# A two-layer graph network kernel: no clearing of the accumulator by GpSimd, seventeen groups gathered from x, and a longer ring of row buffers

## The chip, the cores and the metric

The kernel runs on one core of one Trainium2 chip, as one program. The metric is device microseconds of one execution; the chip's engines are TensorE (PE), VectorE (DVE), ScalarE (ACT), GpSimd (POOL) and SyncE (SP), and DMAs are issued from the queues of SP, ScalarE and GpSimd. Times of before are the median of three executions; the profile is one further execution.

## The reference

There are N = 12,500 nodes of 128 float32 features and 200,000 edges, sorted by their destination `dst`. Cut to what matters:

```
h     = relu(layernorm(x))
w     = edge_weight / segment_sum(edge_weight, dst)[dst]
feat  = relu(h @ W_pool + b_pool)
neigh = segment_max(feat[src] * w, dst)           # layer 1: largest message
r     = h @ W1_self + neigh @ W1_neigh + b1
h1    = relu(r / norm(r))
neigh2 = segment_sum(h1[src] * w, dst) / max(deg, 1)   # layer 2: mean of messages
out   = x + relu(h1 @ W2_self + neigh2 @ W2_neigh + b2)
```

Nodes without edges get 0 in place of the maximum.

## The kernel before

**Groups.** The edges are taken in 391 groups of G = 512 (the last has 320), each as four chunks of 128. For a chunk GpSimd issues one indirect DMA (`gather`, L446): 128 rows of 512 bytes of a table in HBM, chosen by one column of `srcT`, land in one quarter of a row buffer of 128x4x128 float32. Layer 1 gathers from `feat_d`, layer 2 from `h_d`; both tables are written by the kernel. Since the edges are sorted, a group touches a window of at most LW = 48 consecutive nodes; `bases` holds where each window begins.

**Preparation.** A hand-ordered loop of 28 turns (`tc.manual_schedule()`: the order of the program is the order on each engine) runs over 25 node groups of 4x128 nodes. In turn i it does the statistics of node group i (L571 to L576), the normalised rows `xn` and their transposes for i-1 (L554 to L562), `hT` and the product with `W_pool` for i-2 (L546 to L550), and `feat` for i-3, with its store to `feat_d` from SP (L541, L542). The rows of x are loaded into `agg` itself, seen as `xs`; once the rows of a node group are read, GpSimd sets these columns to zero (L563), since `agg` is later the accumulator over nodes. In between, the turns carry steps of three side jobs: `edges1` for the first quarter of the edges, `sources` (turns the source numbers, which lie in `w2T`, into `srcT`; first quarter in turns 0 and 1, the rest in turns 9 to 14) and the loads of the other inputs.

**Raw groups.** `feat_d` is complete only at the end of the preparation. So the first FIRST = 14 groups are gathered from x, which is there from the start: two or three chunks in each turn from turn 2 on, after the turn's clearing. These groups are turned into features on the way (`raw_stats`, `raw_norm`, `raw_columns`, `raw_back`, `raw_product`), at a cost in VectorE, ScalarE and TensorE.

**Layer 1.** A loop of one step per group: ScalarE scales the gathered rows (L868), TensorE transposes them (L869), VectorE takes the running maximum along the edges with a scan (L877), picks the last edge of each node (L885, L886), and a product with a selection matrix (L897, L926) gives 48 columns which ScalarE copies into `agg` at the window's place (`window_copy`, L819). When all windows of 128 nodes are in, `nodes1` computes their `h` and stores it to `h_d`. From step FIRST on, two of three steps also take a `side_step`, which carries on the jobs of `background()`: `edges1` for the other quarters, then `edges2`, `edges3` and `fitness`. `fitness` writes flags into `bad`; where one is set, a slow general path runs at the end of the kernel.

**Row loads beside the gathers.** For every tenth group (sixth in layer 2) `Rows` loads the first chunk row by row with 128 DMAs of 512 bytes from SP and ScalarE (L689), whose addresses come from a small tile `ri` (L672 to L685).

**The ring.** A gather waits until its row buffer has been read. There are RING = 8 own buffers and 8 borrowed ones in tiles that are filled only later: two in `locT`, one each in `lastT` and `invT`, four in `w2T`. Layer 1 uses all 16 for groups below LESS = 64 and the first 8 from there on; layer 2 uses 8. On VectorE's queue and ScalarE's, step i's work waits for the gather of group i; GpSimd's queue is a list of gathers that runs ahead of the steps by as much as the ring lets it.

**Small tiles.** `work(name)` gives single tiles `r_<name>`. The keep flags of groups 0 and 1 lie in `r_f1` (`kt_first`) and the edge weights of group 0 in `r_f0` (`w_first`) until steps 0 to 2 have read them.

Of the kernel before, what the change touches and what calls it, by code (L numbers as in the profile page):

```python
# [7 lines left out]
F32 = mybir.dt.float32  # L8
# [5 lines left out]
OP = mybir.AluOpType  # L14
# [4 lines left out]
P = 128  # L19
D = 128  # L20
G = 512
Q = 4
LW = 48
# [6 lines left out]
ROW_SHIFT = 9  # L30
BL = 8
XC = 8
FIRST = 14
RING = 8
WIDE = 2 * RING
LESS = 64


@with_exitstack
def gnn_kernel(ctx, tc, x, src, dst, ew, w_pool, b_pool, w1s, w1n, b1, w2s, w2n, b2, out):  # L40
# [13 lines left out]
    nc = tc.nc  # L54
    N = x.shape[0]
# [6 lines left out]
    NT = -(-NG // P)  # L62
# [12 lines left out]
    agg = const.tile([P, NP + LW], F32)  # L75
    srcT = const.tile([P, NT, Q, P], I32)
    ewT = const.tile([P, NT, Q, P], F32)
# [12 lines left out]
    rp = both.enter_context(tc.tile_pool(name="rows", bufs=1))  # L90
# [17 lines left out]


    ring = [gp.tile([P, Q, D], F32, name=f"gt{k}") for k in range(RING)]  # L110
    lent = locT.bitcast(F32)
    ring += [lent[:, t:t + 2].rearrange("p t q n -> p (t q n)").rearrange("p (q d) -> p q d", d=D) for t in (0, 2)]
    ring += [a[:, 2:4].rearrange("p t q n -> p (t q) n") for a in (lastT, invT)]
    ring += [w2T[:, t] for t in range(NT)]
    assert len(ring) == WIDE and LESS % WIDE == 0

    def buffer(g, wide):
        return ring[g % (WIDE if wide and g < LESS else RING)]


    dr = rp.tile([P, NT, G + 2], I32)
# [22 lines left out]
    xs = agg[:, :NP].rearrange("p (t d) -> p t d", d=D)  # L144
# [55 lines left out]
    sums = rp.tile([P, NT + 2], F32)  # L200
    counts = rp.tile([P, NT + 2], F32)
    heads = rp.tile([P, NT + 2], F32)
    bad = rp.tile([P, NT, 5], F32)
    for tl in (sums, counts, heads):
        nc.vector.memset(tl, 0.0)
    ones_r = rp.tile([P, G], BF16)
# [2 lines left out]
    def work(name, n=G, dtype=F32):  # L209
        return rp.tile([P, n], dtype, name=f"r_{name}")  # L210
# [27 lines left out]
    def at_pairs(out, f, op):  # L238
        nc.vector.tensor_reduce(out, pairs(f), axis=AX.X, op=op)
# [135 lines left out]
    def fitness(get, t):  # L375

        before, cur, behind = (dr[:, t, i:i + G] for i in range(3))
        begin = work("first", 1)
        nc.vector.tensor_copy(begin, cur[:, 0:1])
        pn = beside(get, cur)  # L380
        yield
        wrong = work("goes", dtype=BF16)
        nc.vector.tensor_tensor(wrong, pn, before, OP.is_lt)
        yield
        nc.vector.tensor_reduce(bad[:, t, 0:1], wrong, axis=AX.X, op=OP.max)
        yield
        loc = work("f1")
        nc.vector.tensor_scalar(loc, pn, float(N - 1), begin, op0=OP.min, op1=OP.subtract)
        last = work("last", dtype=BF16)
        yield  # L390
        nc.vector.tensor_tensor(last, pn, behind, OP.not_equal)
        yield
        nc.vector.tensor_scalar(wrong, loc, float(LW - 1), None, op0=OP.is_gt)
        yield
        nc.vector.tensor_reduce(bad[:, t, 1:2], wrong, axis=AX.X, op=OP.max)
        yield

        one = work("one", 1)
        nc.vector.tensor_tensor(one, before[:, 0:1], behind[:, G - 1:G], OP.is_equal)
        real = work("real", 1)  # L400
        nc.vector.tensor_scalar(real, begin, float(PAST), None, op0=OP.is_lt)
        nc.vector.tensor_tensor(bad[:, t, 2:3], one, real, OP.mult)
        nc.vector.tensor_tensor(bad[:, t, 3:4], begin, need[:, t:t + 1], OP.is_lt)
        yield

        at_pairs(loc[:, :G // 2], last, OP.min)
        yield
        nc.vector.tensor_reduce(bad[:, t, 4:5], loc[:, :G // 2], axis=AX.X, op=OP.max)
# [29 lines left out]
        ne = G if g < GF else TAIL  # L438
        return *divmod(g, P), ne, [(j, min(P, ne - j * P)) for j in range(-(-ne // P))]

    def gather(gt, table_d, g, byrow=None, only=None):
        t, r, ne, chunks = edges_of(g)
        for j, k in chunks if only is None else chunks[only:only + 1]:
            if j == 0 and byrow and byrow.takes(g):
                continue
            nc.gpsimd.indirect_dma_start(  # L446
                out=gt[:k, j, :], out_offset=None, in_=table_d[:, :],
                in_offset=bass.IndirectOffsetOnAxis(ap=srcT[:k, t, j, r:r + 1], axis=0))
        return gt


    gts = {}
# [43 lines left out]
    rest = load_rest()  # L496
    groups = list(node_groups())
    offs, rstds, pts, pfs = ({} for _ in range(4))
    raw_chunks = [(r, j) for r in range(FIRST) for j in range(Q)]

    def split_bias():

# [29 lines left out]
    for i in range(len(groups) + 3):  # L532
        at = [groups[i - k] if 0 <= i - k < len(groups) else None for k in range(4)]
        if at[3]:
            t0, n = at[3]
            pf = pfs.pop(i - 3)
            fr = wk.tile([P, Q, D], F32, name="fr", bufs=3)
            if i % 4 == 3:
                nc.scalar.activation(fr[:, :n, :], pf[:, :n, :], AF.Relu)
            else:  # L540
                nc.vector.tensor_scalar(fr[:, :n, :], pf[:, :n, :], 0.0, None, op0=OP.max)  # L541
            nc.sync.dma_start(feat_d[t0 * P:(t0 + n) * P, :].rearrange("(q p) d -> p q d", p=P),  # L542
                              fr[:, :n, :])
        if at[2]:
            t0, n = at[2]
            nc.scalar.activation(hT[:, t0:t0 + n, :], pts.pop(i - 2)[:, :n, :], AF.Copy)  # L546
            pf = pfs[i - 2] = ps.tile([P, Q, D], F32, name="pf")
            nc.tensor.matmul(pf[:, :n, :], ones_r[0:3, :P], bias_rows[0:3, :n, :], start=True, stop=False)
            for q in range(n):
                nc.tensor.matmul(pf[:, q, :], hT[:, t0 + q, :], W["pool"], start=False, stop=q == n - 1)  # L550
        if at[1]:
            t0, n = at[1]
            rstd = rstds.pop(i - 1)
            nc.vector.reciprocal(rstd, rstd)  # L554
            off = wk.tile([P, Q], F32, name="off")
            nc.vector.tensor_tensor(off, offs.pop(i - 1), rstd, OP.mult)
            xn = wk.tile([P, Q, D], F32, name="xn")
            pt = pts[i - 1] = ps.tile([P, Q, P], F32, name="pt")
            for q in range(n):
                nc.scalar.activation(xn[:, q, :], xs[:, t0 + q, :], AF.Relu, bias=off[:, q:q + 1],  # L560
                                     scale=rstd[:, q:q + 1])
                nc.tensor.transpose(pt[:, q, :], xn[:, q, :], ident)  # L562
            nc.gpsimd.memset(xs[:, t0:t0 + n, :], 0.0)  # L563
        if at[0]:
            t0, n = at[0]
            mv = wk.tile([P, Q, 2], F32, name="mv")
            if n < Q:
                nc.vector.memset(mv, 1.0)
            for q in range(n):
                st = wk.tile([P, 6], F32, name="st")  # L570
                nc.vector.bn_stats(st, xs[:, t0 + q, :])  # L571
                nc.vector.bn_aggr(mv[:, q, :], st)
            rstd = rstds[i] = wk.tile([P, Q], F32, name="rstd")
            nc.scalar.activation(rstd, mv[:, :, 1], AF.Sqrt, bias=eps)
            offs[i] = ps.tile([P, Q], F32, name="neg")
            nc.vector.tensor_scalar(offs[i], mv[:, :, 0], -1.0, None, op0=OP.mult)  # L576
        if 2 <= i < 22:
            next(first_edges, None)
        if i >= 6:
            next(rest, None)  # L580
        if i == 1:
            bias_rows = split_bias()
        if i < 2 or 9 <= i < 15:
            next(source_steps, None)
        if i >= 2:
            n = 2 + (i % 4 == 2) if i < len(groups) else len(raw_chunks)
            for r, j in raw_chunks[:n]:
                gts[r] = gather(buffer(r, True), x, r, only=j)
            raw_chunks = raw_chunks[n:]
        if i == len(groups) - 1:  # L590
            w_first, kt_first = (rp.tile([P, G], F32, name=f"r_f{k}") for k in range(2))
            kt_first = kt_first.bitcast(BF16).rearrange("p (two n) -> p two n", two=2)
            weight_rows(0, w_first)
            keep_rows(0, kt_first)
        k = i - len(groups)
        if k == 1:
            raw_scale(0)
            raw_norm(0)
            raw_columns(pq, 0)
        if k == 2:  # L600
            raw_back(0)
            raw_product(pq, 0)
            nc.scalar.activation(gts[0], raws.pop(0), AF.Relu, bias=bp_col)
            raw_scale(1)
            raw_norm(1)
        if 0 <= k < 3:
            raw_stats(k)
# [180 lines left out]
    with tc.manual_schedule(), tc.tile_pool(name="ew", bufs=3) as wk, \  # L788
# [47 lines left out]
        byrow = Rows(wk, feat_d, 10, [(nc.sync, 96, 16), (nc.scalar, 32, 4)], 30, NG - 16)  # L836
        for i in range(max(turn) + 6):
# [23 lines left out]
            elif i < NG:  # L861
                t, r, ne, chunks = edges_of(i)
                gs = wk.tile([P, G], F32, name="gs", bufs=2).rearrange("p (q d) -> p q d", d=D)
                pms[i] = ps.tile([P, G], F32, name="pm")
                gt = gts.pop(i)
# [7 lines left out]
            g = i - 1  # L873
            if 0 <= g < NG:
# [3 lines left out]
                                             op0=OP.add, op1=OP.max)  # L878
# [13 lines left out]
            g = i - 3  # L892
            if 0 <= g < NG:
                t, r, ne, chunks = pairs_of(g)
# [14 lines left out]
            g = i - 2  # L909
# [7 lines left out]
            g = i - 4  # L917
# [25 lines left out]
        i = NG  # L943
# [172 lines left out]
```

## Time and profile before

| | us |
|---|---|
| median of three executions | 5949.51 (5947.85 to 5975.21) |
| the profiled execution, its own time | 3844.75 |
| its span | 3843.0 |
| last store of `feat_d` issued / first gather from `feat_d` | 96.6 / 101.9 |
| last gather of layer 1 / first of layer 2 | 1940.3 / 1957.9 |
| GpSimd busy | 2873.2, in 3061 instructions |

The profiled execution is far shorter than the timed ones; the page and the trace don't show why. Its mean granted TensorE clock was 0.52: near full in the first 100 us, 0.50 from 600 us on. In the page each digit of a row of slices is the busy share of a fortieth of the span in tenths. A group of instructions is told by line, engine, operation, result and operands, its count, busy time in sum and mean of one in ns, then the idle time of that engine just before and what ended it. An indirect DMA's busy time on GpSimd is the time in which GpSimd handles it; when its data land is seen at those who wait for them.

### The profile page before, as it was taken

Reading aid. Unit: us, or ns where it says so; the run is one execution under the profiler, and the core shown is the slowest. Engines: PE = TensorE matmul, PEld = TensorE weight load, DVE = VectorE, ACT = ScalarE, POOL = GpSimd, SP = SyncE. Lnnn points to the kernel's source line nnn. Section 1 sums busy time; section 2 is a strip of 40 time slices with the busy share of each in tenths; the row PEclk is TensorE's granted clock in tenths of the full one; section 3 lists DMA queues with packets and bytes.
Section 4 is the critical chain, followed back from the end, with each engine's and each line's share of the span. In section 5 each row is a group of like instructions: output and inputs, shape, how many; then the busy total and the mean of one; then the engine's idle time right before and its main releaser. Section 6 shows DMA issues by size and latency. Waiting matters only on the chain.

```text
span 3843.0 us, 61269 instructions
## 1 busy us (share of the span) xinstructions
PE 2317.6 (60%) x8402; PEld 1790.5 (47%) x8402; DVE 1712.7 (45%) x4882; ACT 882.9 (23%) x2996; POOL 2873.2 (75%) x3061
## 2 busy tenths in 40 slices
PE   7666566666666666666655555555555555555555
PEld 5455454444444444444444444444444444444444
DVE  8877666666666666555542222222222222222221
ACT  7644444444444444444410000000000000000000
POOL 6777777777777777777767777777777777777776
PEclk9655555555555555555555555555555555555555
DMA  7433333323333333333312222222222222222222
GB/s 204 122 91 90 87 89 89 89 83 84 86 86 86 86 86 85 85 85 85 84 52 63 62 64 62 62 63 63 63 63 63 62 63 63 63 63 63 63 63 57
DMA packets 224215, 299.55 MB, mean 78 GB/s; under 512 B 70418, under 2 KB 147444, under 8 KB 223798
## 3 DMA queue, kind: packets, MB, share of 16 engines
q0 software_dynamic: 96864, 198.51, 19.8%
q1 hardware_dynamic: 115766, 93.43, 8.5%
q10 hardware_dynamic: 11168, 3.61, 0.6%
q14 instruction: 345, 2.83, 0.2%
q8 instruction: 72, 1.18, 0.1%
HBM read 275.50 MB, written 19.77 MB: 77 GB/s over the span
## 4 chain that ended last, share of the span: by engine, by line
DMA 55%; issue 11%; POOL 8%; PE 7%; DVE 6%; SPq 5%; ACT 4%; ACTq 3%; POOLq 0%; DVEq 0%
DMA gt<-h_d,srcT 33%; DMA gt<-feat_d,srcT 20%; POOL gt L446 8%; PE pa L985 3%; SPq L689 3%; ACTq L689 2%; ACT gs L868 2%; DVE pm L877 2%; PE pm L869 1%; SPq L685 1%; PE pn L739 1%; ACTq L685 1%; PE pn L735 1%; DVE sc L886 1%; DVE sel L897 1%
## 5 line engine op out<-in xcount | busy, mean ns | idle before, releaser
L446 POOL DMA_INDIRECT gt<-h_d,srcT x1499 | 1415.3, 944 | 474.1 <-issue 217.6
L446 POOL DMA_INDIRECT gt<-feat_d,srcT x1371 | 1295.2, 945 | 418.3 <-DMA gt<-feat_d,srcT 165.4
L985 PE MATMUL pa<-s,gt 128*128 128x48 f32 x2998 | 962.3, 425 | 809.2 <-DMA gt<-h_d,srcT 730.4
L985 PEld LDWEIGHTS pa<-s,gt 128*128 128x128 f32 x2998 | 749.7, 312 | 1024.3 <-DMA gt<-h_d,srcT 812.3
L869 PE MATMUL pm<-ident,gs 128*128 128x128 f32 x1507 | 573.0, 463 | 640.2 <-ACT gs L868 557.3
L877 DVE TENSOR_TENSOR_SCAN pm<-kt,carry,pm 128x512 f32<-128x512 bf16 x389 | 499.7, 1285 | 480.7 <-PE pm L869 473.7
L869 PEld LDWEIGHTS pm<-ident,gs 128*128 128x128 f32 x1507 | 284.0, 193 | 877.4 <-ACT gs L868 742.6
L994 DVE TENSOR_TENSOR agg<-pa,agg 128x48 f32 x391 | 81.2, 208 | 1351.6 <-PE pa L985 950.2
L868 ACT ACTIVATE gs<-gt,ewT 128x128 f32<-128x128 f32 x1371 | 489.6, 395 | 584.9 <-DMA gt<-feat_d,srcT 433.6
L926 PEld LDWEIGHTS pa<-sel,rows 128*128 128x128 f32 x1556 | 365.8, 324 | 51.7 <-ACT agg L819 51.3
L926 PE MATMUL pa<-sel,rows 128*128 128x48 f32 x1556 | 369.1, 385 | 17.1 <-ACT agg L819 16.4
L914 PE MATMUL pr<-ident,sc 128*128 128x128 f32 x782 | 243.7, 414 | 0.0
L897 DVE TENSOR_SCALAR sel<-cols,lastT,invT 128x48 f32<-128x48 f32 x782 | 211.0, 323 | 0.0
L886 DVE COPY_PREDICATED sc<-kt,pm 128x256 f32<-128x256 int16 x389 | 172.0, 442 | 13.2
L914 PEld LDWEIGHTS pr<-ident,sc 128*128 128x128 f32 x782 | 168.8, 225 | 0.1
L885 DVE COPY sc<-pm 128x256 f32<-128x256 f32 x391 | 162.0, 414 | 0.0
L967 DVE TENSOR_TENSOR s<-hit,w2T 128x192 f32<-128x192 f32 x391 | 139.8, 357 | 13.5
L904 ACT ACTIVATE rows<-pr 128x256 f32<-128x256 f32 x392 | 142.6, 364 | 0.5 <-PE pr L914 0.5
L965 DVE TENSOR_TENSOR hit<-iota,locT 128x192 f32<-128x192 f32 x391 | 140.4, 359 | 1.1
L819 ACT ACTIVATE agg<-pa 128x48 f32 x389 | 79.0, 203 | 180.5 <-PE pn L735 175.9
L675 DVE TENSOR_SCALAR ri<-ri 1x128 int32<-1x128 int32 x99 | 25.3, 256 | 196.9 <-DMA ri<-in_src 195.8
L739 PE MATMUL pn<-w_2s,hT 128*128 128x128 f32 x196 | 74.2, 483 | 0.0
(228 smaller groups left out, 1685.4 us busy)
## 6 DMA issues: line engine op xcount, KB each, us to landing
ga<-h_d SPq DMA_DIRECT2D x4096, 0.5 KB
ga<-h_d ACTq DMA_DIRECT2D x4096, 0.5 KB
ga<-feat_d SPq DMA_DIRECT2D x3360, 0.5 KB
kt<-keep_d SPq DMA_DIRECT2D x194, 256.0 KB
gt<-h_d,srcT POOLq DMA_INDIRECT x1499
gt<-feat_d,srcT POOLq DMA_INDIRECT x1371
ga<-feat_d ACTq DMA_DIRECT2D x1120, 0.5 KB
h_d<-h SPq DMA_DIRECT2D x98, 64.0 KB
```

Source lines behind the costliest of these rows:

```text
L446: nc.gpsimd.indirect_dma_start(out=gt[:k, j, :], out_offset=None, in_=table_d[:, :], in_offset=bass.IndirectOffsetOnAxis(ap=srcT[:k, t, j, ...
L689: row = eng.dma_start(ga[r + k:r + k + 1, :], self.bytes[None, bass.ds(at[k], 4 * D)])
L868: nc.scalar.activation(gs[:k, j, :], rows_j, AF.Copy, scale=ewT[:k, t, j, r:r + 1])
L869: nc.tensor.transpose(pms[i][:, j * P:j * P + k], gs[:k, j, :], ident[:k, :k])
L877: nc.vector.tensor_tensor_scan(pm[:, :ne], kt[:, :ne], pm[:, :ne], carry, op0=OP.add, op1=OP.max)
L885: nc.vector.tensor_copy(sc[:, :ne // 2], two[:, :, 1])
L886: nc.vector.copy_predicated(sc[:, :ne // 2], new[:, :, 1], two[:, :, 0])
L897: nc.vector.tensor_scalar(sels[g][:k, j, :], cols[:k, 1, :], lastT[:k, t, j, r:r + 1], invT[:k, t, j, r:r + 1], op0=OP.is_equal, op1=OP.mult)
L904: nc.scalar.activation(rws[g][:k, j, :], pr[:k, j, :], AF.Copy)
L914: nc.tensor.transpose(prs[g][:k, j, :], sc[:, j * P:j * P + k], ident)
L926: nc.tensor.matmul(pas[g], rows[:k, j, :], sel[:k, j, :], start=j == 0, stop=j == len(chunks) - 1)
L985: nc.tensor.matmul(pas[g], rows_j, s[:k, j, :], start=j == 0, stop=j == len(chunks) - 1)
```

## The change

- The clearing of `xs` by GpSimd (L563) goes. Only the first 48 columns of `agg` are set to zero, by VectorE in turn 15. So columns that no window covers would keep rows of x; `fitness` gets two more flags, which are set where a group's node range lies further than LW from its neighbours', and `bad` grows from 5 to 7 columns.
- FIRST is 17 in place of 14: three more groups come from x and are treated as raw groups. The gathers of raw groups 0 to 13 are all issued in turn 1, those of 14 to 16 in turn 15 (their buffers are in `w2T`, which holds the sources until turn 14).
- The ring has 18 buffers (two quarters of `ewT` are added); groups 18, 19 and 20 lie in `r_f0`, `r_f1` and a third quarter of `ewT`. The 18 serve groups up to 56, 14 of them the 56 groups from 57 to 112, and 8 the rest.

```diff
-FIRST = 14
+FIRST = 17
 RING = 8
-WIDE = 2 * RING
-LESS = 64
+WIDE = 18
+LESS = 3 * WIDE
+MID = 14
+LEAST = LESS + 4 * MID
...
     ring = [gp.tile([P, Q, D], F32, name=f"gt{k}") for k in range(RING)]
+    ring += [ewT[:, t] for t in (2, 3)]
...
+    mid = ring[:RING] + ring[RING + 2:RING + 4] + ring[-NT:]
...
     def buffer(g, wide):
-        return ring[g % (WIDE if wide and g < LESS else RING)]
+        if not wide:
+            return ring[g % RING]
+        if WIDE <= g < WIDE + 3:
+            k = g - WIDE
+            return (work(f"f{k}").rearrange("p (q d) -> p q d", d=D) if k < 2 else ewT[:, 1])
+        h = g if g < WIDE else g - 3
+        if h < LESS:
+            return ring[h % WIDE]
+        return mid[(h - LESS) % MID] if h < LEAST else ring[(h - LEAST) % RING]
...
+        after = work("after", 1)
+        nc.vector.tensor_scalar(after, behind[:, G - 1:G], float(N), begin, op0=OP.min, op1=OP.subtract)
+        nc.vector.tensor_scalar(bad[:, t, 5:6], after, float(LW), None, op0=OP.is_gt)
+        nc.vector.tensor_tensor(after, begin, before[:, 0:1], OP.subtract)
+        nc.vector.tensor_scalar(bad[:, t, 6:7], after, float(LW), None, op0=OP.is_gt)
+        yield
...
-            nc.gpsimd.memset(xs[:, t0:t0 + n, :], 0.0)
...
-        if i >= 2:
-            n = 2 + (i % 4 == 2) if i < len(groups) else len(raw_chunks)
-            for r, j in raw_chunks[:n]:
-                gts[r] = gather(buffer(r, True), x, r, only=j)
-            raw_chunks = raw_chunks[n:]
+        if i == 15:
+            nc.vector.memset(agg[:, :LW], 0.0)
+        if i in (1, 15):
+            for r in range(FIRST):
+                if (r < WIDE - NT) == (i == 1):
+                    gts[r] = gather(buffer(r, True), x, r)
```

More of the change, by code (lines that the diff above doesn't have):

```diff
@@ L114, in gnn_kernel @@
     ring += [w2T[:, t] for t in range(NT)]
-    assert len(ring) == WIDE and LESS % WIDE == 0
+    mid = ring[:RING] + ring[RING + 2:RING + 4] + ring[-NT:]
+    assert len(ring) == WIDE and len(mid) == MID and FIRST < WIDE
     def buffer(g, wide):
-        return ring[g % (WIDE if wide and g < LESS else RING)]
+        if not wide:
[7 more added lines that the diff above has]
+        return mid[(h - LESS) % MID] if h < LEAST else ring[(h - LEAST) % RING]
     dr = rp.tile([P, NT, G + 2], I32)
@@ L202, in gnn_kernel @@
     heads = rp.tile([P, NT + 2], F32)
-    bad = rp.tile([P, NT, 5], F32)
+    bad = rp.tile([P, NT, 7], F32)
     for tl in (sums, counts, heads):
@@ L439, in edges_of, with gather @@
         return *divmod(g, P), ne, [(j, min(P, ne - j * P)) for j in range(-(-ne // P))]
-    def gather(gt, table_d, g, byrow=None, only=None):
+    def gather(gt, table_d, g, byrow=None):
         t, r, ne, chunks = edges_of(g)
-        for j, k in chunks if only is None else chunks[only:only + 1]:
+        for j, k in chunks:
             if j == 0 and byrow and byrow.takes(g):
@@ L498, in gnn_kernel @@
     offs, rstds, pts, pfs = ({} for _ in range(4))
-    raw_chunks = [(r, j) for r in range(FIRST) for j in range(Q)]
     def split_bias():
```

## The prediction

> **What bounds the kernel now.** I read the page from its totals to the slices, then GpSimd's list of groups, then its order of time.
>
> ```profile
> span 3843.0 us, 61269 instructions
> PE 2317.6 (60%) x8402; PEld 1790.5 (47%) x8402; DVE 1712.7 (45%) x4882; ACT 882.9 (23%) x2996; POOL 2873.2 (75%) x3061
> ...
> POOL 6777777777777777777767777777777777777776
> ```
>
> No engine is full, but GpSimd's digit is flat at 7 while the others' digits change from stage to stage. Its groups say why (line, engine, operation, names, count, then busy and mean, then idle):
>
> ```profile
> L446 POOL DMA_INDIRECT gt<-h_d,srcT x1499 | 1415.3, 944 | 474.1 <-issue 217.6 <-PE pa L985 119.7 <-DMA gt<-h_d,srcT 108.7
> L446 POOL DMA_INDIRECT gt<-feat_d,srcT x1371 | 1295.2, 945 | 418.3 <-DMA gt<-feat_d,srcT 165.4 <-issue 149.8 <-ACT gs L868 60.1
> L563 POOL MEMSET agg<- 128x512 f32 (+1 forms) x25 | 13.3, 533 | 20.0 <-ACT xn L560 14.3 <-DMA feat_d<-fr 5.6
> ```
>
> A gather is 0.944 us busy and 474.1/1499 = 0.32 us idle: a period of 1.25 us. The windows of 100 us hold 81 GpSimd instructions each from 100 us to 1900, so 75.6% busy is this engine at its full pace. The releasers after 0.3 us are only what ended last in that fixed gap. The chain that ended last says "DMA gt" for 53%: the gathers' arrivals, which follow GpSimd's issue. So after the head the time is (gathers that are left) x 1.25 us, plus the turn between the layers (first h_d gather at 1957.9, last feat_d one at 1940.3) and the tail. The head is the place of the change; GpSimd in order of time (start, duration):
>
> ```profile
> 10.11 0.52 POOL L563 MEMSET agg<- 128x512 f32 x1 [8.62 <-ACT xn L560]
> 15.07 0.53 POOL L563 MEMSET agg<- 128x512 f32 x1 [4.45 <-ACT xn L560]
> 15.77 1.11 POOL L446 DMA_INDIRECT gt<-in_x,srcT  x1 [0.17 <-issue]
> ...
> 34.42 0.53 POOL L563 MEMSET agg<- 128x512 f32 x1 [5.55 <-DMA feat_d<-fr]
> ...
> 100.66 0.94 POOL L446 DMA_INDIRECT w2T<-in_x,srcT  x1 [0.30 <-issue]
> 101.90 0.94 POOL L446 DMA_INDIRECT w2T<-feat_d,srcT  x1 [0.30 <-issue]
> ```
>
> The first feat_d gather follows the last x gather after the usual 0.30 us: it did not wait for feat_d. The head is set by GpSimd's own list, in which each clearing stands ahead of two or three gathers and holds them until ScalarE has read the columns.
>
> **What the Trainium skill says.** "Perfetto Trace Analysis", section "DMA Instruction — SWDGE (GPSIMD)", says that the profiled end of such a DMA is the end of descriptor generation, not of the data. The trace agrees: gathers follow each other at 1.25 us, whether the data are waited for or not. "SBUF — State Buffer", section "Who interferes with whom", says that VectorE operations of one input in a two-port mode and GpSimd block each other. The gathers show no such stretch (903 to 1315 ns, median 944), so I count nothing for VectorE when the clearings go.
>
> **The change, part by part** (the profiled execution's clock; its own time is 3844.75, 1.75 around the span).
>
> 1. *25 clearings leave GpSimd.* 41.45 clears, 42.15 gathers, where the gather before began at 40.50: 1.65 us between gathers instead of 1.25, so 0.40 each, 10 us in all. Their waits leave too: 5.55 us at 28.9 to 34.4 and the start. The indices srcT are ready at 10.21 + 0.58 = 10.8, the first gather goes at 15.77 now and at about 11.0 then: 4.8. One clearing of 128x48 on VectorE is added at turn 15: the 0.13 us of GpSimd's own 128x48 (L191) bounds it above; 0.1, in a stage in which VectorE is 89% busy (55.88 of 63 us): 0 to 0.1.
>
> 2. *56 gathers at once, then 12.* From 11.0: 56 x 1.25 = 70, to 81. The 12 of groups 14 to 16 go to w2T, which holds the sources until the fourth srcT write (60.1): free long before. 12 x 1.25 = 15, to 96. Before, group 17's first gather would stand at 101.9 + 3 x 4 x 1.25 = 116.9; GpSimd alone would bring it to 96, 20.9 earlier.
>
> 3. *What is late next: feat_d.* The last store of it is issued by 91.24 + 5.40 = 96.64 on SP. An uncontended store's landing is not listed; the chain has one of 2.16 us at 83.51. So feat_d is there at about 98.9 and is now what releases the first feat_d gather. The earlier gathers also meet the x loads: at 11 to 34 us the DMA engines are full (297 GB/s). By 34 us there are 18 gathers instead of 12. All gathers took 19.8% of 16 engines' span, 761 us over 2926 = 0.26 us each: 6 x 0.26 = 1.6 us later x, and everything after it by as much. Bounds: nothing (the engines' order absorbs it) and 4 us (twice the bytes' share, since small packets). I take 1.6: first feat_d gather at 100.5, so 16.4 gained.
>
> 4. *A new wait at group 19.* It writes f1, where the keep rows of groups 0 and 1 lie until the copy at 110.58 + 0.44 = 111.0, with 1.6 later 112.6, +0.1. Its turn comes at 100.5 + 10 = 110.5. About 2.1 us are lost; behind it only gathers are queued on GpSimd. Group 18's f0 is free at the product of step 0 (100.68 + 0.70 = 101.4, + 1.6), before its turn at 105.5; group 20's ewT and 21's first buffer likewise. So group 20 starts at 117.6 instead of 131.9: **14.3 us gained**.
>
> 5. *Three more raw steps.* Scans of raw steps come every 5.55 us (119.41, 124.95, 130.50), of gathered ones in a run about 3.1 (186.22, 189.55, 192.74, 195.35). So consumption of group 17 and later is 3 x 2.45 = 7.3 later, + 1.6 = 8.9. Scan 30 stands at 230.1 and group 30's gather at 181.8, so that lateness costs nothing while a buffer is there. Cover: GpSimd's lead.
>
> 6. *The ring.* With gathers 14.3 earlier and consumption 8.9 later the lead grows by 23.2 us, 4.7 groups. I laid the gathers' starts of before against the scan of the group that used the buffer, with both shifts. Smallest slack: about 4 us at group 71 (over 57, the first lap of 14), then 6 at 72; after the return to 8 about 6 at 125. Before, the shrink to 8 at group 64 leaves about nothing at 65 and then 5 or more. Nothing is lost; were consumption 4 us later still, about that much would be lost once, not per group. The moved gathers pass nothing but clearings and each other on GpSimd's queue; SP keeps its order and gets one 256 KB load of weight rows for each of the three raw steps (0.43 issue each), while the lead covers them. The background steps begin at turn 17 instead of 14; at two in three turns their some 200 steps end near turn 320 of 391, so 70 turns cover that.
>
> 7. *The flag.* Four 128x1 operations and a wider reduction for each of 4 jobs: 4 x (4 x 0.17) = 2.7 us of VectorE (0.17 from the 128x4 operations L554, L576), at steps where VectorE is 63% busy and waits for the gathers. 0; 3 if the cover were gone.
>
> Sum in the profiled execution: -14.3, bounds -9 (x loads 4 late, a longer wait at 19, ring) and -17.5 (no x delay, no wait at 19): about 3830.5.
>
> **To the median.** The runs shown have a median of 5949.51, 2104.8 more than the profiled execution, 1.547 of it. No view shows where that time is. If all stretches alike, 14.3 is 22.1. If only GpSimd's periods stretch (2105 over 2926 gathers is 0.72 each), x gathers end after feat_d is ready, parts 3 and 4 fall away and the 4.8 at the start and 25 x 0.40 x 1.55 = 15.5 are gained: 20.3. If the excess is apart from this, 14.3. I take the mean of the first two and a little for the waits in part 1: -23.
>
> **The rivals.** About 0.5% (30 us) is what a measurement of this kernel can tell from no change.
> - *A, the forecast: the head's gain arrives, -9 to -33.* For it: the flat 75.6% of GpSimd, and the missing wait at 101.90. Time 5926. Chance 0.44, of it 0.38 within 0.5% and 0.06 above (waits of part 1 that stretch too).
> - *B: the head is GpSimd's own in the runs as well and stretches in whole.* The 20.9 of part 2, not cut by feat_d, times 1.547 is 32.3: 5917; more if the clearings stretch more than the gathers or waits for ScalarE grow. For it: a slower GpSimd is the simplest reading of 2105 us. Against: feat_d would have to come early. 0.34, faster by over 0.5%.
> - *C: consumption is the bound in the runs: slower.* The row-by-row loads on SP (L689) already make consumption cycle in 43.8 us for ten groups (gaps before the scans at 221.5, 265.3, 309.6), against 48.7 of GpSimd. If they stretch by over 1.11 more than GpSimd, an early gather is worth nothing and the raw steps' 8.9 are paid: x 1.547 is 13.8, 5963. Over 0.5% if a raw step (PE, ScalarE and VectorE in turn) stretches to about three times a gathered one, 3 x 10 us. Against: in the profile GpSimd never waits. 0.17, of which 0.13 over 0.5%.
> - *D: no effect:* the gathers at turn 1 are held by something else, feat_d at 101.9 as before, and POOL's list only shifts: the three groups still save 15 less what the x loads lose; near 5940. 0.05.
>
> So faster 0.34 + 0.06 = 0.40, same 0.38 + 0.04 + 0.05 = 0.47, slower 0.13. The time is A's, 5949.5 - 23 = 5926. Low 5890: B with its gain not quite doubled, as the stretch's place is unknown. High 5964: C within 0.5%; C's upper part is left out, and a little below. A's own range is 5916 to 5940.
>
> **What would show it.** Right: the first x gather at 11, the 68th by 96 to 98, no L563; the first feat_d gather, for group 17, at 99 to 102 with a wait for feat_d; one wait of 1 to 3 us ahead of the gather into r_f; then 81 per 100 us; the turn to h_d 14 us earlier. Wrong: a first feat_d gather after 105 (x loads), GpSimd waits for ACT gs L868 well above 0.3 us near group 71 or 125 (ring), or a profiled time shorter by 14 with an unmoved median (C).

## The result and the profile after

The changed kernel took 6011.48 us in the median (5997.70 to 6023.38), the kernel before 5957.73 on the same chip: **1.0085 times before, 95% interval 1.007 to 1.010**, some 51 us slower where 23 us less was forecast (14 in the profiled execution). The profiled execution that the prediction read (3844.75 us) is unlike every timed one of before, so before was profiled once more (5971.11 us), and the traces below are compared with that one. The page of after, its totals and GpSimd's row of slices:

```profile
span 6006.1 us, 61273 instructions
...
PE 1965.9 (33%) x8408; PEld 1711.2 (28%) x8408; DVE 1692.3 (28%) x4932; ACT 857.4 (14%) x3005; POOL 2865.2 (48%) x3036
...
POOL 4554453544544454455454444444454444444443
```

The same lines of before, profiled again:

```profile
span 5969.3 us, 61269 instructions
...
PE 1966.5 (33%) x8402; PEld 1711.9 (29%) x8402; DVE 1681.5 (28%) x4882; ACT 851.0 (14%) x2996; POOL 2872.5 (48%) x3061
...
POOL 6653444444444444444444444444444444444443
```

GpSimd is busy for 48% in both, not at its full pace of 75.6%. The two rows differ most at the start: 4 against 6 in the first slice. So the view that carried the prediction, a flat 7, does not hold in the timed runs. GpSimd's groups of after say what it waits for (busy, mean ns | idle before it, by releaser):

```profile
L465 POOL DMA_INDIRECT gt<-h_d,srcT x1499 | 1417.6, 946 | 1594.3 <-PE pa L1003 956.3 <-issue 370.0 <-remote 200.1
L465 POOL DMA_INDIRECT gt<-feat_d,srcT x1273 | 1205.3, 947 | 1239.8 <-ACT gs L886 854.9 <-issue 330.3 <-ACT rows L922 28.2
```

In layer 2 only 0.25 us a gather (370.0/1499) is its own gap. Of the 1594 us of waiting, 956 are for TensorE to have read a row buffer, and of the 1240 in layer 1, 855 are for ScalarE to have done so. So where GpSimd waits for its readers, a gather issued early is worth nothing by itself. The waits of after, longest sums, say what the readers wait for (us, times, longest):

```profile
DVE ri L693 <- DMA ri<-in_src: 2005.6, 84, 35.1
PEld pa L1003 <- DVE s L985: 1798.8, 86, 48.2
```

VectorE stands 2006 us for the row numbers of the row-by-row loads, as in before (1961 us), and TensorE stands for VectorE's selections `s`. The head is where after loses; GpSimd in order of time:

```profile
11.07 1.12 POOL L465 DMA_INDIRECT gt<-in_x,srcT  x1 [9.59 <-ACT srcT L452]
12.50 0.95 POOL L465 DMA_INDIRECT gt<-in_x,srcT  x1 [0.30 <-issue]
...
85.06 0.95 POOL L465 DMA_INDIRECT w2T<-in_x,srcT  x1 [0.31 <-issue]
106.19 0.95 POOL L465 DMA_INDIRECT w2T<-in_x,srcT  x1 [20.18 <-DVE sf L449]
...
116.34 0.95 POOL L465 DMA_INDIRECT w2T<-in_x,srcT  x1 [0.30 <-issue]
160.22 0.94 POOL L465 DMA_INDIRECT w2T<-feat_d,srcT  x1 [42.94 <-issue]
...
172.43 0.95 POOL L465 DMA_INDIRECT r_f<-feat_d,srcT  x1 [2.51 <-DVE sc L904]
```

From 11 to 86 us the gathers of x run without a gap, as forecast. Then GpSimd stands, and the first gather from `feat_d` goes at 160.2. In before, profiled again, it went here:

```profile
107.91 0.94 POOL L446 DMA_INDIRECT w2T<-in_x,srcT  x1 [0.30 <-issue]
110.97 0.94 POOL L446 DMA_INDIRECT w2T<-feat_d,srcT  x1 [2.11 <-issue]
```

49 us lie between them. Gathers that save nothing later have only moved; what moved with them is the work behind. The scan of group 18 starts at 292 us in after and at 236 in before, and at the end of the run the kernels are still 37 us apart in these two profiles.

What stood still? Order of time in after for the other engines and SP, while GpSimd gathers:

```profile
26.60 2.07 PE L568 MATMUL pf<-w_pool,hT 128*128 128x128 f32 x8 [7.59 <-issue]
...
35.01 50.83 SPq L560 DMA_DIRECT2D feat_d<-fr  x3
49.05 0.69 DVE L559 TENSOR_SCALAR fr<-pf 128x512 f32<-128x512 f32 x1 [24.68 <-remote]
...
60.90 2.07 PE L568 MATMUL pf<-w_pool,hT 128*128 128x128 f32 x8 [30.84 <-issue]
...
62.77 1.06 PE L580 MATMUL pt<-ident,xn 128*128 128x128 f32 x4
...
84.75 0.69 DVE L559 TENSOR_SCALAR fr<-pf 128x512 f32<-128x512 f32 x1 [32.28 <-remote]
...
94.55 0.60 ACT L564 ACTIVATE hT<-pt 128x512 f32<-128x512 f32 x1 [31.97 <-remote]
```

TensorE finishes a product `pf` at 28.67, and VectorE, whose instruction waits for TensorE's semaphore alone, starts at 49.05; the next `pf` is done at 62.97 and is taken at 84.75. That is 20.4 and 21.8 us late. ScalarE takes the transposes `pt`, done at 63.83, at 94.55, 30.7 us late. ("remote" is the page's word for a releaser that it cannot place.) In before, profiled again, a `pf` that is done at 38.28 is taken at 38.31. The line of SP joins three stores, spread over 50.83 us: the last two follow VectorE's `fr` of 49.05 and 84.75. From 11 to 86 us the preparation does two turns. In the first 100 us TensorE is busy for 20.6 us, against 67.6 in before. Full DMA engines are not what holds the signals up: from 34 to 86 us they are 22% busy in after and 55% in before, profiled again.

The trace also records when each semaphore moves. Taking the time from the end of each TensorE instruction that raises one to the next record of that semaphore: in after the median is 0.01 us where GpSimd has been idle for 1.5 us, 0.65 in the second gather of a run without gaps, 1.67 in the sixth to tenth. Beyond the twentieth it is 20.9, but that is ten signals in two places, five of them at 63 us, in the stall above. Before, profiled again, shows the same steps (0.01, 0.64, 1.71), but no signal of TensorE falls beyond the twentieth gather of a run there. In its 3845 us execution it is 0.01 us everywhere, even deep inside runs of over twenty. Nor does the length of a run alone set the delay: in e4_before_norows, below, 15 signals beyond the twentieth gather have a median of 3.4 us. Some records are missing (about a quarter of TensorE's), so these are upper bounds; the late starts of VectorE and ScalarE above need no such record.

### The profile page after: what moved, and what is told of

Same layout as the page of the kernel before. It is cut to its first block, busy times and chain, and to the rows that moved or that the text cites. A ratio compares the mean times of both kernels' runs of the same rounds, so it can differ in the third digit from the quotient of the medians.

```text
span 6006.1 us, 61273 instructions
## 1 busy us (share of the span) xinstructions
PE 1965.9 (33%) x8408; PEld 1711.2 (28%) x8408; DVE 1692.3 (28%) x4932; ACT 857.4 (14%) x3005; POOL 2865.2 (48%) x3036
## 5 line engine op out<-in xcount | busy, mean ns | idle before, releaser
L465 POOL DMA_INDIRECT gt<-feat_d,srcT x1273 | 1205.3, 947 | 1239.8 <-ACT gs L886 854.9
L1003 PE MATMUL pa<-s,gt 128*128 128x48 f32 x2998 | 681.9, 410 | 1820.4 <-DVE s L985 1785.0
L1003 PEld LDWEIGHTS pa<-s,gt 128*128 128x128 f32 x2998 | 666.1, 332 | 1835.7 <-DVE s L985 1798.8
L887 PE MATMUL pm<-ident,gs 128*128 128x128 f32 x1495 | 453.9, 445 | 999.8 <-DVE sc L904 352.4
L886 ACT ACTIVATE gs<-gt,ewT 128x128 f32<-128x128 f32 x1273 | 407.5, 392 | 189.0 <-issue 187.0
L465 POOL DMA_INDIRECT w2T<-feat_d,srcT x98 | 92.7, 945 | 124.2 <-issue 67.1
```

Of the source, the lines that this page charges most:

```text
L465: nc.gpsimd.indirect_dma_start(out=gt[:k, j, :], out_offset=None, in_=table_d[:, :], in_offset=bass.IndirectOffsetOnAxis(ap=srcT[:k, t, j, ...
L886: nc.scalar.activation(gs[:k, j, :], rows_j, AF.Copy, scale=ewT[:k, t, j, r:r + 1])
L887: nc.tensor.transpose(pms[i][:, j * P:j * P + k], gs[:k, j, :], ident[:k, :k])
L1003: nc.tensor.matmul(pas[g], rows_j, s[:k, j, :], start=j == 0, stop=j == len(chunks) - 1)
```

## The experiments

**Theory S**: while GpSimd's gathers follow each other without a gap, the other engines' signals (their semaphores) arrive late; the clearings, which waited for ScalarE in every turn, had kept the run short. **Theory R**: the ring or the three raw groups cost the time. **Theory C** is the prediction's rival: the row loads set the pace. Each ratio is to runs of before on the same chip.

| kernel | median, us | ratio to before (95%) | first `feat_d` gather, us |
|---|---|---|---|
| after | 6011.48 | 1.0085 (1.007 to 1.010) | 160.2 |
| e1_spread | 6009.81 | 1.0080 (1.0051 to 1.0108) | 158.6 |
| e2_burst | 5998.87 | 1.0059 (1.0039 to 1.0079) | 150.2 |
| e5_before | 5962.81 | 1.0006 (0.9992 to 1.0019) | 111.0 |
| e6_noclear | 5991.50 | 1.0051 (1.0034 to 1.0067) | 151.4 |
| e7_paced | 5979.86 | 1.0037 (1.0024 to 1.0051) | 127.4 |
| e9_ring | 5959.20 | 1.0008 (0.9990 to 1.0026) | 108.8 |
| e10_flag | 5949.20 | 0.9999 (0.9983 to 1.0015) | 112.6 |
| e11_noclear_tick | 5989.69 | 1.0059 (1.0036 to 1.0083) | 151.4 |
| e13_raw17 | 6077.63 | 1.0036 (1.0015 to 1.0056) | 125.9 |
| e14_raw11 | 6074.36 | 1.0046 (1.0029 to 1.0062) | 112.3 |
| e15_gate14 | 6048.00 | 0.9997 (0.9984 to 1.0011) | 113.0 |
| e3_after_norows | 4680.98 | 0.7852 (0.7825 to 0.7879) | 163.1 |
| e4_before_norows | 4656.66 | 0.7809 (0.7783 to 0.7835) | 109.3 |
| e8_paced_norows | 4648.45 | 0.7805 (0.7790 to 0.7820) | 125.4 |
| e12_norows_tick | 4653.58 | 0.7822 (0.7797 to 0.7847) | 110.2 |
| e16_raw11_norows | 4723.75 | 0.7807 (0.7788 to 0.7826) | 112.9 |

(The chip of e13 to e16 was slower: before took 6052.36 us on it.)

### Where the gathers of x stand

**e1_spread**: after, with the raw gathers two or three a turn in program order, as before has them.

```diff
-        if i in (1, 15):
-            for r in range(FIRST): ...
+        if i >= 2:
+            n = 2 + (i % 4 == 2) if i < len(groups) else len(raw_chunks)
+            for r, j in raw_chunks[:n]:
+                gts[r] = gather(buffer(r, True), x, r, only=j)
```

> The kernel after, with the gathers of raw groups issued two or three to a turn from turn 2 on as before (those left over in turn 25), and all else as after. Theory S (GpSimd's gathers, when they follow each other without a gap, hold back the DMAs that SP issues; the run of 60 gathers at the head makes the feat_d stores late): the stores of feat_d go at the pace of before, the first feat_d gather stands 40 to 60 us earlier than its 160.2 in the kernel after, the time is 5945 to 5975, 0.7 to 1.1% under after. Rival R (the three more raw steps and the later consumption cost the 50 us): the head gets shorter, but the time stays within 15 us of after's 6011.

No change against after: theory S's forecast missed. The trace shows why. With no clearing between them nothing on GpSimd's queue waits for the turn, so the gathers ran back to back just the same. Place in a program's order is no pacing.

**e2_burst**: before with its clearings, but raw groups 0 to 11 gathered in turn 1 and 12 and 13 in turn 15.

> The kernel before, with the gathers of raw groups 0 to 11 all issued in turn 1 and those of 12 and 13 in turn 15; clearings, 14 raw groups and the ring of 16 then 8 stay. Theory S: about 48 gathers run without a gap from 11 to 71 us, the stores of feat_d are held as in the kernel after, first feat_d gather near 150, time 35 to 60 us over before (+0.6 to +1.0%). Rival R: within 15 us of before. A third theory, that clearing by GpSimd mattered in itself: no forecast of a change here.

35 us slower (0.0059 x 5963), `feat_d` 39 us later than in e5_before: the unbroken run alone, with ring, flag and 14 raw groups as before, brings the stall.

### What the clearings did

**e5_before**: before, unchanged.

> The kernel before, unchanged, profiled once more, because its first profiled execution (3844.75 us) was far shorter than its timed runs (5957.73 us) and so shows neither their stalls nor their order. Expected if the profile is like the timed runs: span about 5950 us, row loads at some 0.7 us each beside gathers instead of 0.32, other engines' semaphore signals seen up to some microseconds late while GpSimd gathers without a gap (as in the runs without row loads), and in the head feat_d's stores ending near 100 to 106 us and its first gather at 105 to 112 us. Rival (the head of before has the same stall as that of after): first feat_d gather near 150 to 160 us.

The first forecast came true: `feat_d`'s first gather at 111.0. Its rival, a stall in before's own head, is out.

**e6_noclear**: before without the clearings.

```diff
-            nc.gpsimd.memset(xs[:, t0:t0 + n, :], 0.0)
+        if i == 15:
+            nc.vector.memset(agg[:, :LW], 0.0)
```

> Before with the 25 clearings of xs left out (VectorE clears 48 columns of agg instead, as after does), everything else as before: 14 raw groups issued two or three chunks a turn in program order, old ring. Theory S (GpSimd's unbroken run of gathers holds back the other engines' signals, and the clearings, which wait for ScalarE each turn, were what broke the run): the gathers run back to back from 11 us to about 70, feat_d's stores end 30 to 45 us later than in before, first feat_d gather at 140 to 155 us, and the time is 25 to 45 us over before. Rival (the three further raw groups or the ring of 18, 14 and 8 buffers cost the time): first feat_d gather within 5 us of before and the time within 10 us of it.

Order of time, SP (three stores, the last far behind the first) and GpSimd:

```profile
35.03 47.34 SPq L542 DMA_DIRECT2D feat_d<-fr  x3
```

```profile
151.41 0.94 POOL L446 DMA_INDIRECT w2T<-feat_d,srcT  x1 [48.55 <-issue]
```

Taking away 10 us of work on GpSimd costs 30 us (20 to 40). This one edit is over half of after's loss.

**e11_noclear_tick**: the same, with one GpSimd instruction a turn that waits for nobody, a memset of 128x1 ahead of the turn's gathers.

```diff
+            nc.gpsimd.memset(tick, 0.0)
```

> The kernel without clearings, with one GpSimd memset of 128x1 (0.10 us) a turn between the raw gathers that waits for nobody. It tells what in the clearings let the other engines' signals through. Theory T (any GpSimd instruction that issues no descriptors between two gathers lets them through): head near that of before, first feat_d gather at 105 to 120 us, time within 12 us of before. Rival W (only time in which GpSimd waits does): head as without clearings, first feat_d gather at 145 to 155 us, time 25 to 45 us over before.

```profile
13.64 0.94 POOL L447 DMA_INDIRECT gt<-in_x,srcT  x1 [0.30 <-issue]
14.59 0.12 POOL L589 MEMSET tick<- 128x1 f32 x1
14.89 0.94 POOL L447 DMA_INDIRECT gt<-in_x,srcT  x1 [0.19 <-issue]
```

The small memset fits into the 0.30 us between two gathers, which stay 1.25 us apart. (From 64 us on five of the memsets show waits of 0.4 to 2.4 us, which this kernel was not meant to have.) VectorE takes the products `pf` at 47.58 and 81.18 us, in e6_noclear at 47.68 and 81.28: the same stall. So the clearing's own place on the queue was not what helped.

**e15_gate14**: before with each clearing cut to one column, which still waits for ScalarE (0.10 us instead of about 0.53; the 48 columns as in e6_noclear).

```diff
-            nc.gpsimd.memset(xs[:, t0:t0 + n, :], 0.0)
+            nc.gpsimd.memset(xs[:, t0, 0:1], 0.0)
```

> Before with its 25 clearings cut to one column of xs a turn (0.10 us instead of 0.40), VectorE clearing the 48 columns of agg: the gate of the paced kernel with the 14 raw groups and ring of before. If waiting for ScalarE is all that the clearings did, the time is within 10 us of before. Rival (the gate is worse than the clearing, by itself): 15 to 30 us over before.

Level with before (0.9997). e6, e11 and e15 together: what matters is **that GpSimd waits** once a turn, not what it does there. e15 also removes most of the clearing's busy time and gains nothing by it.

**e7_paced**: after with that one-column gate and the gathers of e1_spread.

> After, with its 17 raw groups issued two or three chunks a turn and one GpSimd clearing a turn of a single column of xs once that turn's rows were read, so that GpSimd waits for ScalarE each turn as it did in before; ring and flag as in after. Theory S: the head is that of before again, first feat_d gather at 112 to 122 us instead of 160, and the time is within 15 us of before, some 35 to 60 us under after. Rival (ring, raw groups or flag): the time stays within 15 us of after's 6011, whatever the head does.

```profile
24.60 0.10 POOL L582 MEMSET agg<- 128x1 f32 x1 [1.17 <-ACT xn L579]
24.85 0.94 POOL L465 DMA_INDIRECT gt<-in_x,srcT  x1
26.09 0.94 POOL L465 DMA_INDIRECT gt<-in_x,srcT  x1 [0.30 <-issue]
34.05 0.10 POOL L582 MEMSET agg<- 128x1 f32 x1 [7.01 <-ACT xn L579]
```

The head is restored (127.4, after twelve more x gathers than before), and about 29 us of after's 51 come back (0.0085 - 0.0037 = 0.0048). It missed its own bound of 15 us: about 22 stay.

The lateness can be laid beside the waits. In each of 25 turns take the time by which VectorE or ScalarE starts on `pf` after TensorE has finished it and the engine itself is free. The longest of a run is 21.8 us in after, 21.8 in e1, 19.7 in each of e2, e6 and e11, where the gathers run on; it is 7.0 in e5, 6.2 in e7 and 5.0 in e15, where GpSimd waits once a turn (and 5.2 in before's 3845 us execution).

### What stays: ring, flag, raw groups

**e9_ring**: the new `ring`, `mid` and `buffer`, nothing else. **e10_flag**: the two flag columns, nothing else.

> Before with the ring of after alone (18, then 14, then 8 row buffers); 14 raw groups, the clearings and the flag stay as in before. The paced kernel left 23 us over before unexplained. Theory R (the ring: groups up to 113 in 14 buffers let GpSimd run ahead without a gap for longer, so that signals are held back, or borrowed buffers come free later): 10 to 30 us over before. Rival (the ring is neutral and the rest of 23 us is the raw groups' or the flag's): within 8 us of before.

> Before with the two further flag columns alone: 40 more VectorE operations of one element a partition in the background steps. Prediction's step 7: nothing, within 8 us of before. Rival (background steps are not hidden when VectorE's signals come late): 8 to 25 us over before.

Neither differs from before. The ring is not quite idle, though: in e9_ring the gathers run without a gap from 109 to 168 us (33 of them from 110 to 150, against 28 in e5_before), the scans of groups 2, 3 and 4 lie some 23 us apart there (129.2, 152.3, 174.7; in e5_before 132.2, 146.7, 152.3), and that of group 8 starts at 197 us instead of 174. By group 139 the two are 5 us apart (1117 and 1112), so it was given back.

**e13_raw17**: e9_ring with `FIRST = 17`. **e14_raw11**: before with `FIRST = 11`.

> Before with the ring of after and 17 raw groups instead of 14; clearings and flag as in before. The ring alone measured +5 us or less. Theory G (each raw group costs some 7 us more than the gathers of x save, because in the timed runs the consumers and not GpSimd set the pace): 15 to 30 us over before. Rival (the 23 us of the paced kernel came from its gate): within 10 us of before. The prediction's step 2 and 5 would have it faster by some 14 us.

> Before with 11 raw groups instead of 14, all else as in before. Theory G: 15 to 30 us under before. Rival (raw groups are neutral beyond the clearings): within 10 us of before. By the prediction's own reasoning (a raw group's four gathers start during the preparation and save GpSimd time) 10 to 20 us over before.

Last x gather and first `feat_d` gather of e13_raw17, and the same place in e14_raw11 and e15_gate14 (14 raw groups, same chip):

```profile
124.63 0.94 POOL L458 DMA_INDIRECT w2T<-in_x,srcT  x1 [0.30 <-issue]
125.88 0.94 POOL L458 DMA_INDIRECT w2T<-feat_d,srcT  x1 [0.30 <-issue]
```

```profile
104.96 0.31 POOL L563 MEMSET agg<- 128x256 f32 x1 [2.32 <-ACT xn L560]
112.32 0.95 POOL L446 DMA_INDIRECT invT<-feat_d,srcT  x1 [7.05 <-issue]
```

```profile
110.25 0.94 POOL L446 DMA_INDIRECT w2T<-in_x,srcT  x1 [0.30 <-issue]
113.04 0.94 POOL L446 DMA_INDIRECT w2T<-feat_d,srcT  x1 [1.85 <-issue]
```

17 raw groups cost 22 us (9 to 34), what e7_paced had left. 11 cost 28 (18 to 38), so theory G, a price for each raw group, falls. With 14, `feat_d` is there just when the x gathers end (1.85 us of waiting). With 17, GpSimd is still busy with x at 125: group 17's first gather would stand at 113.0 + 12 x 1.25 = 128 with 14 raw groups, so only 2 us are gained, and the three groups still go the longer raw way. The scans show it: group 17's starts at 266 us in e13_raw17 and at 228 in e15_gate14. Part of that is the ring's (254 in e9_ring, on a faster chip), which is given back; at group 139 the two are still 21 us apart (1145 and 1124). With 11, GpSimd waits for `feat_d` after 44 gathers of x and starts on group 11 when it could have been at group 14. That the raw way itself makes up the 22 us is argued from these times; no run took it apart from the gathers.

### The row loads

**e3_after_norows, e4_before_norows**: `Rows` takes no group; GpSimd gathers every chunk.

```diff
         def takes(self, g):
-            return g % self.every == 0 and self.first <= g < self.end
+            return False
```

> The kernel after without the loads row by row: GpSimd gathers every chunk of every group in both layers. Theory S says that in the timed runs these loads on SP (period 0.73 to 1 us beside gathers, 0.32 alone) set the pace from group 30 on, not GpSimd: without them GpSimd is the bound, 1495 + 1563 gathers x 1.25 = 3822 us + head 160 + turn 20 + tail 12: about 4015. If GpSimd's own pace is what makes the timed runs long (B of the prediction), 100 more gathers make it about 200 us longer than after.

> The kernel before without the loads row by row, as e3. Theory S: GpSimd-bound, 1507 + 1563 gathers x 1.25 = 3838 + head 102 to 130 + 32: 3970 to 4000. So before stays 15 to 45 us ahead of after here too, by the late feat_d of the head less the 15 us of three groups. Rival R (raw steps and late consumption cost the time in after): where GpSimd is the bound these are covered, and after is 10 to 20 us ahead of before.

Without row loads **before takes 4657 us, 22% less than with them**, with 99 more gathers. Three lines of after in SP's order of time show how fast they go (start, time for so many rows):

```profile
1003.52 20.18 SPq L707 DMA_DIRECT2D ga<-feat_d  x16
1026.06 12.71 SPq L707 DMA_DIRECT2D ga<-feat_d  x16
1041.60 12.29 SPq L707 DMA_DIRECT2D ga<-feat_d  x32
```

In the first line, most of it beside gathers, 16 rows take 20.18 us; in the third, with GpSimd idle, 32 take 12.29. Over the whole run SP's rows follow each other after 0.322 us in the median where GpSimd has been idle for 0.6 us, and after 0.73 (mean 0.98) beside gathers; 0.74 (0.99) in e5_before, 0.322 in the median in the short execution, beside gathers. The time fell by 1306 us and not by the 2000 expected; late signals have a part in what is left, as this stretch of e4_before_norows shows in order of time; how large a part is not shown:

```profile
3520.48 1.94 PE L977 MATMUL pa<-s,gt 128*128 128x48 f32 x8 [4.31 <-DVE s L959]
...
3529.95 0.94 POOL L446 DMA_INDIRECT gt<-h_d,srcT  x1 [0.30 <-issue]
3531.19 0.94 POOL L446 DMA_INDIRECT gt<-h_d,srcT  x1 [0.30 <-issue]
3531.50 0.21 DVE L986 TENSOR_TENSOR agg<-pa,agg 128x48 f32 x1 [11.07 <-remote]
```

`pa` is complete at 3522.42 and VectorE takes it at 3531.50, in a stretch where all gathers are 1.25 us apart. After keeps its loss without row loads (24 us, 0.43% of before), so the loss does not need them. The forecast of rival R, after ahead of before, failed, but it took GpSimd for the bound, and GpSimd is 64% busy in e4_before_norows, short of its 75.6%.

**e8_paced_norows, e12_norows_tick, e16_raw11_norows**: three tries on that base (the paced kernel; a 128x1 memset after each group's gathers; 11 raw groups).

> The same kernel as the paced one, with no row fetched by SyncE row by row: GpSimd gathers every chunk. Theory S: about 20 to 40 us under after without row loads (4681), so 4640 to 4665, level with before without row loads (4657) to 15 us faster. Rival (ring, raw groups or flag): 4670 to 4695. It is also the candidate for a version that beats both kernels, since row loads cost 1280 to 1330 us.

> Before without row loads (4657 us), with one GpSimd memset of 128x1 (0.10 us) after each group's four gathers in both layers: 782 more instructions, at most some 150 us of GpSimd with their gaps. Theory T (it lets signals through): the 390 and 300 us that GpSimd stood idle in the two layers shrink, and the time falls by 50 to 300 us. Rival W (only waiting lets them through, and GpSimd waits there already): the same to 150 us more, 4650 to 4810.

> Before with 11 raw groups and without row loads. Without row loads GpSimd has the longer work again, so Theory G gives less here: 0 to 15 us under before without row loads (4657). Rival (GpSimd bound, as the prediction reckoned): 5 to 15 us over it.

The paced one undoes after's loss there too (4681 to 4648); against e4_before_norows all three are level within their intervals. So the 22 us of three more raw groups do not show here, though the intervals, 9 to 16 us either way, could hide a part of them. The memset let hardly more signals through: VectorE's `agg` waits for "remote" were 1448 us, against 1525. Any of e4, e8 and e16 beats both kernels by some 22%.

## Why the prediction was wrong, point by point

1. *Clearings leave GpSimd.* Right on GpSimd's list: first x gather at 11.07 (11.0 forecast), then no gap. Wrong on what a clearing was: 0.40 us and a wait were counted as cost, and the wait was the useful part. It held GpSimd back once a turn.
2. *56 gathers at once, then 12.* The first 60 ended at 86.0, on the forecast line (81 for 56). The last 8 waited for the sources, whose turns were late with the preparation: done at 117, not 96.
3. ***Late next: feat_d.* This is the step that failed.** It shifted the preparation by the x loads alone, 1.6 us with 0 to 4 as bounds, and kept its pace beside a run of gathers. The first `feat_d` gather came at 160.2 instead of 100.5. The mis-sized term is the effect of GpSimd's run on the others: about 50 us in the head (160.2 against 111.0), of which e6_noclear and e2_burst show 30 and 35 us in the time of the kernel. The Trainium skill's page "SBUF — State Buffer", section "Who interferes with whom", was read for ports, and it says that TensorE and ScalarE wait for nobody there. Nothing here contradicts that for ports; it was the signals that came late, and the reading of gather durations (944 ns) could not show it. (By 34 us before has issued 9 gathers, not the 12 of the sum, so its term would be 2.3 us; that is within its bounds and changes nothing.) My own "wrong" sign, a first `feat_d` gather after 105, is what came, but not by the x loads that I named for it.
4. *Wait at group 19.* 2.51 us ahead of the gather into `r_f`, 2.1 forecast. The wait came as foreseen, and is of no weight. (The sum without x delay and wait is 14.3 + 1.6 + 2.1 = 18.0, not the 17.5 given as its bound.)
5. *Three more raw steps,* covered by GpSimd's lead. No: GpSimd waits for its readers for most of its 52% idle time, so the reader's time counts. With clearings kept, the three groups cost 22 us (9 to 34). With the 30 of the clearings that makes 52, which is after's loss of 51; the closeness is partly luck, since each interval is some 10 us wide on either side.
6. *Ring* and 7. *flag: nothing.* Right: +5 us (-6 to 15) and -1 (-10 to 9).
8. *To the median.* Scaling the head by 1.547 fell with the view: in the execution like the timed ones the head of before is stretched only from 101.9 to 111.0. Of the 2105 us that the short execution lacked, leaving the row loads out takes 1306 away.

Rival C had the steady state right, consumption bound by the row loads, and its sign. Its price of 13.8 us was for the raw steps alone, which measured 22; the larger part, the stall of the head, was in no rival. What is left open: by what path a run of gathers delays signals and row loads, what besides the run sets the size of the delay, and why one profiled execution was free of it. No run separated these.

## What to carry to other kernels

An instruction that looks like overhead on one queue may be its pacing: before taking it away, ask what its wait held back, and whom that work delays when it is let loose. Work issued ahead gains only up to the moment its next input is ready; 14 raw groups met that moment, 11 and 17 did not. Check first that the profiled execution is as long as the timed ones: here the bound read from one of 3845 us was not that of 5950.

## What the runs showed that was not expected

- Semaphore signals of TensorE, seen 0.01 us after the instruction when GpSimd is idle, were seen 0.65 us (second gather of a run) and 1.67 us (sixth to tenth) after it in the median, beside gathers 1.25 us apart; both are upper bounds. In the head of after, in a run of 60 gathers, VectorE and ScalarE started 20 to 31 us after the TensorE instruction that they waited for. A 0.1 us GpSimd instruction between gathers does not change that; a wait of GpSimd once a turn does.
- SP's row loads of 512 bytes, 0.322 us apart with GpSimd idle, came 0.73 us apart (mean 0.98) beside such gathers. 12,672 such loads cost 1306 us of 5963; GpSimd took over their rows in 99 gathers.
